# Attention and a quantized feed-forward on one core: two key tiles as one pattern of the matmul queue, and VectorE pinned to the order of the source

## The chip, the cores and the metric

The kernel runs on one NeuronCore of a Trainium2 chip. The metric is the device time of one execution in microseconds (us), the median of three runs. The engines are TensorE (PE in the profile, with its weight loads as PEld), VectorE (DVE), ScalarE (ACT), GpSimd (POOL) and SyncE (SP, which here only issues DMAs). They run side by side and wait for one another through semaphores. TensorE writes its results to PSUM[...]; VectorE and ScalarE read them there.

## What is computed

One transformer block in fp32: attention with 16 heads of 16 values over 4 sequences of 2048 rows, a residual and a layer norm, then a gated feed-forward whose activations and weights are rounded to a 4-bit grid in blocks of 16, a residual and a layer norm.

```python
q, k, v = split_heads(x @ Wq.T), split_heads(x @ Wk.T), split_heads(x @ Wv.T)   # x: 4 x 2048 x 256
attn = softmax(q @ k.T / sqrt(16))
x = layernorm(x + merge_heads(attn @ v) @ Wo.T)
gate, up = fp4(x) @ fp4(w_gate).T, fp4(x) @ fp4(w_up).T                         # 256 -> 704
x = layernorm(x + fp4(silu(gate) * up) @ fp4(w_down).T)                         # 704 -> 256
```

fp4(t) divides each block of 16 by a sixth of its largest absolute value, rounds to the nearest of 0, 0.5, 1, 1.5, 2, 3, 4, 6 with the sign kept, and multiplies back.

## The kernel before

**Tiles.** Attention is split into 64 steps (b, qb, g): one sequence, 512 query rows, four of the 16 heads. A step goes over 16 tiles of 128 keys, so the main loop has 1024 periods, one per key tile. The loop variable n counts periods from -20 to 1025.

**A period.** Three streams are in flight at once, at different steps:

- *maxima* (20 periods ahead, LEAD): scores of 128 queries against 512 keys for all four heads, in two halves i. Each half is two matmuls (the two heads of a pair, in rows 0 to 61 and 64 to 125 of the array) into a tile pm of two PSUM banks, and VectorE takes the row maxima of both (L432).
- *exponentials*: scores of 128 keys against 512 queries, with the row maximum folded in through two extra rows, so 64 rows per head. One matmul and one bank per head (pe); ScalarE takes the exponential of each bank into an SBUF tile e (L466).
- *values* (2 periods behind, LAG): four matmuls of 32 columns, one per head, into one bank av that adds up over the step.

The source's order for TensorE in a period is: both halves of the maxima, the exponentials' matmuls of the first pair, the values, the exponentials' matmuls of the second pair, and then one *part*.

**Parts.** All other work is cut into parts, written as generators: each runs to its next `yield` and gives a cost; a cost of at least 300 (LEAST) uses up the period's budget of one part (two before n = 0). Parts come from `urgent` (max_rows, which turns the maxima into the extra rows: its transposes are called pn; normalize, which divides by the softmax sums: pa, and pr for every second step) and from `queue`. The queue holds, for each block of 512 rows: the output projection (residual, py), the projection of a block of the next sequence (project: transposes ptx, then k and q in pq, v in pv), the transposes of the rounded x (ptq), gate and up (pg, pu), the transposes of the rounded hidden rows (pth) and the down projection (pz). A part that only waits yields LEAST and so uses a turn.

**Steps off TensorE.** `later(periods, step, rest)` puts a step into `due`; `take_due` runs it when its period has come, and a caller can ask whether it was done at least `rest` periods ago. fp4 takes block maxima, scales and multiplies, and rounds one period later; it works on VectorE and GpSimd. layer_norm takes its moments on VectorE (bn_stats, L524) and the rest on GpSimd.

**Order.** Every matmul and transpose is pinned to the source's order by `tc.keep_in_program_order`. Instructions of the other engines are ordered by the framework's scheduler, by its own estimate of when each is ready. The scheduler also picks the buffer that a tile gets and puts in the waits.

**Banks.** pm has two tiles of two banks (pool ps_m), av one bank (ps_av), and everything else, pe and all parts, shares three banks (pool ps_x, tag px, function psum).

**The end.** After the loop what is left of the parts is drained, and feed_forward_last does the last 512 rows with most of its steps on VectorE (fp4_at_once).

The main loop's core:

```python
for i in range(NP):
    if m < N:
        maxima(sm, im, i)
for i in range(NP):
    if 0 <= n < N:
        exponentials(s, kt, i)
    if i == 0 and n >= LAG:
        values(sv, kv)
...
period(1 if n >= 0 else 2)
```

Of the kernel before, what the change touches and what calls it, by code (L numbers as in the profile page):

```python
# [53 lines left out]
E_BUFS = 10  # L55
# [17 lines left out]

@with_exitstack
def block_kernel(
# [12 lines left out]
    nc = tc.nc  # L88
    B, L, D = x.shape
# [56 lines left out]
    def fp4(pool, t, tag, gain=1.0):  # L146

        p, nb, _ = t.shape
        amax = pool.tile([p, nb], F32, tag="amax" + tag, name="amax")
        nc.vector.tensor_reduce(amax, t, AX.X, ALU.max, apply_absolute_value=True)  # L150
        sc = pool.tile([p, nb], F32, tag="sc" + tag, name="sc")
        nc.vector.tensor_scalar(sc, amax, gain / 6.0, 1e-12, ALU.mult, ALU.max)
        rs = pool.tile([p, nb], F32, tag="rs" + tag, name="rs")
        nc.vector.reciprocal(rs, sc)
        nc.gpsimd.tensor_scalar(rs, rs, gain * TIES_DOWN, 1.0, ALU.mult, ALU.mult)
        xn = pool.tile([p, nb, FB], F32, tag="xn" + tag, name="xn", bufs=3 if tag else 2)
        nc.gpsimd.tensor_tensor(xn, t, rs.unsqueeze(2).to_broadcast([p, nb, FB]), ALU.mult)

        def rounded():
            m = pool.tile([p, nb, FB], F32, tag="m" + tag, name="m", bufs=1)  # L160
            nc.vector.tensor_single_scalar(m.bitcast(I32), xn.bitcast(I32), EXPONENT, ALU.bitwise_and)
            nc.vector.tensor_scalar(m, m, 1.0, ROUND, ALU.max, ALU.mult)  # L162
            nc.gpsimd.tensor_tensor(xn, xn, m, ALU.add)  # L163
            nc.gpsimd.tensor_tensor(xn, xn, m, ALU.subtract)  # L164
            nc.gpsimd.tensor_tensor(xn, xn, sc.unsqueeze(2).to_broadcast([p, nb, FB]), ALU.mult)  # L165

        return xn, later(1, rounded, 4 if tag == "" else 2)

    def fp4_at_once(pool, t, tag, gain=1.0):

        step = nc.vector
        p, nb, _ = t.shape
        amax = pool.tile([p, nb], F32, tag="amax" + tag, name="amax")
        step.tensor_reduce(amax, t, AX.X, ALU.max, apply_absolute_value=True)
        sc = pool.tile([p, nb], F32, tag="sc" + tag, name="sc")
        step.tensor_scalar(sc, amax, gain / 6.0, 1e-12, ALU.mult, ALU.max)
        rs = pool.tile([p, nb], F32, tag="rs" + tag, name="rs")
        step.reciprocal(rs, sc)
        step.tensor_scalar(rs, rs, gain * TIES_DOWN, 1.0, ALU.mult, ALU.mult)
        xn = pool.tile([p, nb, FB], F32, tag="xn" + tag, name="xn", bufs=3 if tag else 2)  # L180
        step.tensor_tensor(xn, t, rs.unsqueeze(2).to_broadcast([p, nb, FB]), ALU.mult)
        m = pool.tile([p, nb, FB], F32, tag="m" + tag, name="m", bufs=1)
        step.tensor_single_scalar(m.bitcast(I32), xn.bitcast(I32), EXPONENT, ALU.bitwise_and)
        step.tensor_scalar(m, m, 1.0, ROUND, ALU.max, ALU.mult)
        step.tensor_tensor(xn, xn, m, ALU.add)
        step.tensor_tensor(xn, xn, m, ALU.subtract)
        step.tensor_tensor(xn, xn, sc.unsqueeze(2).to_broadcast([p, nb, FB]), ALU.mult)
        return xn
# [14 lines left out]
    vt = [const.tile([P, NG, QT // 2, NP, 3 * DH], F32, tag=f"vt{i}", name=f"vt{i}") for i in range(4)]  # L203
# [40 lines left out]
    def turn_w(name, dst):  # L244
        for kc in range(KC):
# [3 lines left out]
            if name == "wv":  # L249
                nc.vector.tensor_copy(dst[:, kc, :], pt[:, :D])  # L250
                continue

            for n in range(KC):
                nc.vector.tensor_copy(
                    dst[:, kc, n * P : (n + 1) * P].rearrange("p (d h) -> p d h", h=NC),
                    pt[:, n * P : (n + 1) * P].rearrange("p (h d) -> p d h", h=NC),
                )
# [7 lines left out]
    def prepare():  # L265
# [10 lines left out]
        yield 500  # L276
# [37 lines left out]
        for piece, after in zip(pieces, pieces[1:] + [None]):  # L314
# [3 lines left out]
            yield 500  # L318
# [14 lines left out]
    def project(b, tb, what):  # L333
# [7 lines left out]
        for kc in range(KC):  # L341
# [4 lines left out]
            yield 600  # L346
        for name, c in [(w[0], int(w[1])) for w in what if w != "v"]:
# [18 lines left out]
        for t in range(QT if "v" in what else 0):  # L366
            v = vt[(tb * 2 + t // 2) % 4]
            pv = psum("pv")
            for kc in range(KC):
                matmul(  # L370
                    pv[:, :D], xT[:, kc, t * P : (t + 1) * P], wvT[:, kc, :], start=(kc == 0), stop=(kc == KC - 1)
                )
            src = pv[:, :D].rearrange("p (g i j d) -> p g i j d", g=NG, i=NP, j=2)
            for j in range(2):
                nc.scalar.copy(v[:, :, t % 2, :, 2 * j * DH : (2 * j + 1) * DH], src[:, :, :, j, :])
            if t % 2:
                t0 = tb * QT + t - 1
                nc.sync.dma_start(
                    vx[b % 2][:, :, t0 : t0 + 2, :].rearrange("g p t c -> p g (t c)"),
                    v.rearrange("p g t i c -> p g (t i c)"),  # L380
                )
            if t == QT - 1:
                projected.add((b, tb, "v"))
            yield 900
# [32 lines left out]
    def maxima(s, n, i):  # L417
# [14 lines left out]
        nc.vector.tensor_reduce(mx_sb[s][:, t, 2 * i : 2 * i + 2, kb], pm, AX.X, ALU.max)  # L432

    def max_rows(s):

        nm = p2.tile([P, QT, HG], F32, tag="nm", name="nm")
        nc.vector.tensor_reduce(nm, mx_sb.pop(s), AX.X, ALU.max, negate=True)
        nh = p2.tile([P, QT, HG, 2], F32R, tag="nh", name="nh")
        nc.vector.tensor_copy(nh[:, :, :, 0], nm)
        nc.vector.tensor_tensor(nh[:, :, :, 1], nm, nh[:, :, :, 0].bitcast(F32), ALU.subtract)  # L440
# [17 lines left out]
    def exponentials(s, kt, i):  # L458
        kb, col = kt // QT, kt % QT * P
        pe = [psum("pe") for _ in range(2)]  # L460
        for j in range(2):
            rows = slice(R * j, R * j + R)
            matmul(pe[j], k_sb[s, i, kb][rows, col : col + P], q_sb[s, i][rows, :], start=True, stop=True)
        for j in range(2):
            e = p1.tile([P, QB], F32, tag="e", name="e", bufs=E_BUFS)
            nc.scalar.activation(e, pe[j], AF.Exp, scale=SCALE)  # L466
            e_sb[s, kt, 2 * i + j] = e
# [15 lines left out]
    def normalize(s):  # L483
# [11 lines left out]
        nc.vector.reciprocal(rd, pairs[:, :, :, 1:3, 0])  # L495
# [3 lines left out]
        for i in range(NP):  # L499
            nc.vector.tensor_tensor(  # L500
# [5 lines left out]
        yield 500  # L506
        if s % 2 == 0:
            return
        yield 0
# [6 lines left out]
        yield 500  # L516


    def layer_norm(r, t0, n):

        mv = p2.tile([P, n, 2], F32, tag="mv", name="mv")
        for t in range(n):
            st = p2.tile([P, 6], F32, tag="st", name="st")
            nc.vector.bn_stats(st, r[:, t0 + t, :])  # L524
            nc.vector.bn_aggr(mv[:, t, :], st)
# [10 lines left out]
    def residual(b, qb, x1, xq):  # L536

        for t in range(QT):
# [10 lines left out]
            if t % 2:  # L549
                layer_norm(x1, t - 1, 2)  # L550
                tiles = x1[:, t - 1 : t + 1].rearrange("p t (b f) -> p (t b) f", f=FB)
                later(3, lambda tiles=tiles: xq.append(fp4(p2, tiles, "")))
# [36 lines left out]
    def turned(hq, tiles, hT):  # L589
# [4 lines left out]
        for t in range(2):  # L594
# [4 lines left out]
            yield 500  # L599
# [8 lines left out]
        yield 500  # L608
# [11 lines left out]
    def feed_forward(b, qb, between):  # L620
# [13 lines left out]
        for kc in range(KC):  # L634
# [5 lines left out]
            yield 500  # L640
        hq = {}

        def gate(t):
# [3 lines left out]
            later(1, lambda: hq.update({t: fp4(p2, blocks, "h", gain=0.5)}))  # L647

        def out_rows(t):
            layer_norm(x1, t, 2)  # L650
            at = slice(qb * QB + t * P, qb * QB + (t + 2) * P)
            nc.sync.dma_start(out[b, at, :].rearrange("(t p) d -> p t d", p=P), x1[:, t : t + 2, :])
# [25 lines left out]
    def feed_forward_last(b, qb, x1):  # L678
# [8 lines left out]
        def moments(t):  # L687
            st = p2.tile([P, 6], F32, tag="st", name="st")
            nc.vector.bn_stats(st, x1[:, t, :])
            mv = p2.tile([P, 4, 2], F32, tag="mv", name="mv")  # L690
            nc.vector.bn_aggr(mv[:, 0, :], st)
# [5 lines left out]
        def normed(t):  # L697
            mv, rstd = norms.pop(t)
            nc.vector.tensor_scalar(
# [3 lines left out]
        def attended(t):  # L703
# [5 lines left out]
            nc.vector.tensor_add(x1[:, t, :], x1[:, t, :], py[:, :D])  # L709
# [30 lines left out]
        def hidden(t):  # L740
            h = p2.tile([P, FF], F32, tag="h", name="h")
            for half, (a, g, u) in enumerate(gates.pop(t)):
                nc.vector.scalar_tensor_tensor(a, a, 1.0, g, ALU.add, ALU.mult)
                nc.vector.tensor_mul(h[:, half * FH : (half + 1) * FH], a, u)
# [23 lines left out]
        def added(t, pz):  # L768
            nc.vector.tensor_add(x1[:, t, :], x1[:, t, :], pz[:, :D])
# [49 lines left out]
    def period(parts):  # L819

        take_due()
# [6 lines left out]
        while parts > 0 and queue:  # L828
            parts -= (part(queue) or 0.0) >= LEAST
# [30 lines left out]
    for n in range(-LEAD, N + LAG):  # L860
        m = n + LEAD
        (sm, im), (s, kt), (sv, kv) = divmod(m, NKT), divmod(n, NKT), divmod(n - LAG, NKT)
# [6 lines left out]
        if n == N - NKT:  # L869
            x1_last = load_last(*steps[-1][:2])  # L870
# [13 lines left out]
        for i in range(NP):  # L884
            if m < N:
                maxima(sm, im, i)
        for i in range(NP):
            if 0 <= n < N:
                exponentials(s, kt, i)
            if i == 0 and n >= LAG:  # L890
                values(sv, kv)
        if m < N and im == NKT - 1:
            urgent.append(max_rows(sm))
        if n >= LAG and kv == NKT - 1:
            urgent.append(normalize(sv))
            if sv % NG == NG - 1 and sv + 1 < len(steps):
                queue.append(chain(*steps[sv][:2]))
        period(1 if n >= 0 else 2)
    banks["more"] = True
    while urgent or queue or due:  # L900
        period(1)
# [33 lines left out]
```

## Time and profile before

| | us |
|---|---|
| median of three runs | 3654.88 |
| lowest, highest | 3651.22, 3658.14 |
| the profiled execution's own time | 3651.45 |
| its span, first to last instruction | 3649.4 |

Its stages, as busy time of each engine in four stretches of the span:

```profile
core 0: us, PE busy (x) PEld busy (x) DVE busy (x) ACT busy (x) POOL busy (x), PEclk, DMA share, GB/s
0.00:110.00 110.00, 85.11 (x414) 54.45 (x414) 61.56 (x64) 45.77 (x120) 16.34 (x32) 0.94 0.69 222
110.00:300.00 190.00, 169.29 (x978) 71.41 (x977) 139.55 (x167) 130.49 (x274) 65.87 (x70) 0.92 0.44 136
300.00:3560.00 3260.00, 3218.46 (x19735) 1431.91 (x19727) 2564.48 (x2950) 2489.53 (x4995) 1160.50 (x1378) 1.00 0.28 85
3560.00:3650.00 90.00, 61.27 (x231) 35.98 (x231) 50.65 (x131) 25.25 (x60) 8.54 (x16) 0.85 0.02 6
```

Each line gives a stretch, its length, and for each engine the time in which it had an instruction running; PEclk is the share of TensorE's full clock that was granted. The first 110 us load and project, up to 300 us the weights of the feed-forward are rounded and transposed beside the first attention steps, from there to 3560 us the pattern repeats for every block of 512 queries (64 periods), and the last 90 us are feed_forward_last. In a timeline each line is a group of like instructions in a row: start, time from the first start to the last end, engine, source line, operation, out<-in, shapes (rows*columns of the array for matmuls), how many. Matmul ends are modelled by the profiler, so starts tell more than lengths. Nearly all matmuls have line L135, that of the helper; the name of the tile tells which they are.

### The profile page before, as it was taken

What the parts mean: (1) busy time and instruction counts of PE and PEld (TensorE: products, weight loads), DVE (VectorE), ACT (ScalarE), POOL (GpSimd) and SP (SyncE); (2) the same over time, 40 slices, a digit from 0 to 9 for tenths busy, and PEclk for the clock granted to TensorE, in tenths of its full rate; (3) what the DMA queues carried; (4) which work ended last, traced back from release to release, by engine and by line L of the source; (5) the groups of instructions that cost most, each with busy time, mean ns of one, the idle gap of its engine ahead of it and who ended that gap; (6) DMA issues with size and microseconds to landing.
All of it is one profiled execution on the core that took longest, in us unless ns stands there. A gap on an engine that the chain in (4) does not pass through costs nothing.

```text
span 3649.4 us, 57772 instructions
## 1 busy us (share of the span) xinstructions
PE 3534.1 (97%) x21348; PEld 1593.8 (44%) x21348; DVE 2816.2 (77%) x3310; ACT 2691.0 (74%) x5446; POOL 1251.3 (34%) x1496
## 2 busy tenths in 40 slices
PE   7889999999999999999999999999999999999996
PEld 5333444444444444444444444444443434444343
DVE  5777778787787778778787787878778787888845
ACT  3677777777777777777777777777777777777772
POOL 1331423434243242424324243342424325142430
PEclk9999999999999999999999999999999999999998
DMA  6533323323232322323223232322322221222100
GB/s 219 164 123 99 119 68 113 89 85 103 82 98 87 105 84 83 116 68 116 85 85 106 80 100 86 97 85 83 109 69 77 67 84 50 86 66 81 57 21 6
DMA packets 190640, 328.39 MB, mean 90 GB/s; under 512 B 24344, under 2 KB 68248, under 8 KB 190360
## 3 DMA queue, kind: packets, MB, share of 16 engines
q1 hardware_dynamic: 188968, 323.39, 29.1%
q8 instruction: 171, 2.80, 0.3%
q10 hardware_dynamic: 1392, 1.31, 0.1%
q14 instruction: 109, 0.89, 0.1%
HBM read 237.04 MB, written 86.51 MB: 89 GB/s over the span
## 4 chain that ended last, share of the span: by engine, by line
PE 82%; DVE 12%; DMA 2%; POOL 2%; issue 1%; ACT 1%; SPq 0%; POOLq 0%; ACTq 0%; DVEq 0%
PE av L135 24%; PE pe L135 18%; PE pm L135 16%; DVE mx L432 9%; PE pz L135 6%; PE pg L135 5%; PE pu L135 5%; PE pq L135 3%; PE pv L135 2%; PE pth L138 1%; PE pa L138 1%; PE py L135 1%; PE pn L138 1%; DMA qx<-qhi 1%; DVE st L524 1%
## 5 line engine op out<-in xcount | busy, mean ns | idle before, releaser
L432 DVE TENSOR_REDUCE mx<-pm 128x2 f32<-128x1024 f32 x2048 | 2408.6, 1217 | 666.5 <-PE pm L135 662.2
L466 ACT ACTIVATE e<-pe 128x512 f32<-128x512 f32 x4096 | 2218.8, 596 | 676.0 <-PE pe L135 670.8
L135 PE MATMUL av<-e,v 128*32 128x512 f32 x8192 | 1098.0, 608 | 4.2 <-DMA v<-vx 4.2
L135 PE MATMUL pe<-q,k 64*128 64x512 f32 x4096 | 1036.4, 456 | 4.9 <-ACT e L466 4.5
L135 PEld LDWEIGHTS pe<-q,k 64*128 64x128 f32 x4096 | 476.6, 184 | 968.5 <-ACT e L466 853.8
L135 PE MATMUL pm<-k,q 62*128 62x512 f32 x4096 | 805.1, 448 | 67.1 <-DVE mx L432 57.5
L135 PEld LDWEIGHTS pm<-k,q 62*128 62x128 f32 x4096 | 346.8, 185 | 382.7 <-DVE mx L432 178.2
L135 PEld LDWEIGHTS av<-e,v 128*32 128x32 f32 x8192 | 162.1, 108 | 335.5 <-issue 312.9
L572 POOL TENSOR_TENSOR a<-a,g 128x352 f32<-128x352 f32 x120 | 112.6, 938 | 494.5 <-ACT a L571 494.5
L135 PE MATMUL pz<-wdT,hT 128*128 128x128 f32 (+1 forms) x1488 | 233.4, 299 | 1.5 <-ACT hT L757 1.5
L617 POOL TENSOR_TENSOR x<-x,read 128x128 f32<-128x128 f32 x120 | 54.8, 456 | 482.2 <-ACT read L143 482.2
L135 PEld LDWEIGHTS pz<-wdT,hT 128*128 128x128 f32 x1488 | 190.5, 193 | 50.5 <-ACT e L466 18.2
L163 POOL TENSOR_TENSOR xn<-xn,m 128x704 f32<-128x704 f32 (+2 forms) x100 | 153.6, 1536 | 153.5 <-DVE m L162 131.6
L586 POOL TENSOR_TENSOR h<-a,u 128x352 f32<-128x352 f32 x120 | 112.4, 937 | 226.0 <-ACT u L585 224.0
L135 PE MATMUL pg<-wgT,xqT 128*128 128x352 f32 x512 | 186.5, 487 | 1.9 <-ACT xqT L720 1.9
L135 PE MATMUL pu<-wuT,xqT 128*128 128x352 f32 x512 | 185.0, 484 | 0.0
L548 POOL TENSOR_TENSOR x<-x,read 128x256 f32<-128x256 f32 x60 | 43.8, 730 | 374.0 <-ACT read L143 374.0
L164 POOL TENSOR_TENSOR xn<-xn,m 128x704 f32<-128x704 f32 (+2 forms) x100 | 153.8, 1538 | 5.4
L165 POOL TENSOR_TENSOR xn<-xn,sc 128x704 f32<-128x704 f32 (+2 forms) x100 | 126.4, 1264 | 7.5
L573 POOL TENSOR_TENSOR a<-a,g 128x352 f32<-128x352 f32 x120 | 113.9, 949 | 9.4
L135 PEld LDWEIGHTS pg<-wgT,xqT 128*128 128x128 f32 x512 | 87.5, 190 | 60.2 <-ACT e L466 19.1
L135 PEld LDWEIGHTS pu<-wuT,xqT 128*128 128x128 f32 x512 | 87.6, 189 | 58.1 <-ACT e L466 20.0
(114 smaller groups left out, 2278.8 us busy)
## 6 DMA issues: line engine op xcount, KB each, us to landing
k<-kx SPq DMA_DIRECT2D x1024, 128.0 KB
v<-vx SPq DMA_DIRECT2D x64, 768.0 KB
q<-qx SPq DMA_DIRECT2D x256, 124.0 KB
kx<-khi SPq DMA_DIRECT2D x64, 256.0 KB
qx<-qhi SPq DMA_DIRECT2D x64, 256.0 KB
vx<-vt SPq DMA_DIRECT2D x32, 384.0 KB
xb<-in_L_attn_x_dram SPq DMA_DIRECT2D x16, 512.0 KB
kx<-klo SPq DMA_DIRECT2D x32, 256.0 KB
```

Source lines behind the costliest of these rows:

```text
L135: tc.keep_in_program_order(nc.tensor.matmul(*args, **kw))
L138: tc.keep_in_program_order(nc.tensor.transpose(*args))
L163: nc.gpsimd.tensor_tensor(xn, xn, m, ALU.add)
L164: nc.gpsimd.tensor_tensor(xn, xn, m, ALU.subtract)
L165: nc.gpsimd.tensor_tensor(xn, xn, sc.unsqueeze(2).to_broadcast([p, nb, FB]), ALU.mult)
L432: nc.vector.tensor_reduce(mx_sb[s][:, t, 2 * i : 2 * i + 2, kb], pm, AX.X, ALU.max)
L466: nc.scalar.activation(e, pe[j], AF.Exp, scale=SCALE)
L548: nc.gpsimd.tensor_add(x1[:, t, :], x1[:, t, :], read(py[:, :D]))
L572: nc.gpsimd.tensor_mul(a, a, g)
L573: nc.gpsimd.tensor_add(a, a, g)
L586: nc.gpsimd.tensor_mul(h[:, cols], a, u)
L617: nc.gpsimd.tensor_add(x1[:, t, cols], x1[:, t, cols], read(pz))
```

## The change

- **One pattern for two periods.** The loop goes in steps of 2, and the order of the two periods is written out in ORDER: m and n are halves of the maxima of the first and second period, e and f the exponentials of one head each, v and w the values, q and r the places for parts. `exponentials` now takes one head instead of a pair.
- **Both parts at q.** `more(2)` runs two parts one after the other at q. A part that yields TIED (the last transposes before matmuls that read them: xT, xqT, hT) ends the run of parts, and what is left of the budget is taken at r. max_rows and normalize run up to their first `yield` where they are begun.
- **VectorE pinned.** `vector = InOrder(tc, nc.vector)` replaces nc.vector everywhere, so every VectorE instruction keeps the source's order. Due steps are taken after m1 and after n1, that is, behind those maxima.
- **Later due times.** fp4 has a step of its own for the scales, one period after the block maxima, and rounds after three periods instead of one; layer_norm in residual and out_rows comes two periods later; the quantization after it four periods later instead of three; that of the hidden rows three instead of one.
- **Buffers and order.** E_BUFS 12 for 10; three staging tiles vt for four; the projection's parts come in the order k0, q0, v, k1, q1 instead of v last; normalize loses one empty `yield`.

```diff
+ORDER = "m0 e0 m1 e1 q e2 n0 e3 v n1 f0 f1 r f2 w f3".split()
+TIED = 500.0
-E_BUFS = 10
+E_BUFS = 12
...
+class InOrder:
+    def __init__(self, tc, engine):
+        self.tc, self.engine = tc, engine
+
+    def __getattr__(self, name):
+        return lambda *args, **kw: self.tc.keep_in_program_order(getattr(self.engine, name)(*args, **kw))
...
+    vector = InOrder(tc, nc.vector)
...
-        return xn, later(1, rounded, 4 if tag == "" else 2)
+        later(1, scaled)
+        return xn, later(3, rounded, 4 if tag == "" else 2)
...
-    def exponentials(s, kt, i):
+    def exponentials(s, kt, h):
+        i, j = divmod(h, 2)
         kb, col = kt // QT, kt % QT * P
-        pe = [psum("pe") for _ in range(2)]
-        for j in range(2):
-            rows = slice(R * j, R * j + R)
-            matmul(pe[j], k_sb[s, i, kb][rows, col : col + P], q_sb[s, i][rows, :], start=True, stop=True)
-        for j in range(2):
-            e = p1.tile([P, QB], F32, tag="e", name="e", bufs=E_BUFS)
-            nc.scalar.activation(e, pe[j], AF.Exp, scale=SCALE)
-            e_sb[s, kt, 2 * i + j] = e
+        pe = psum("pe")
+        rows = slice(R * j, R * j + R)
+        matmul(pe, k_sb[s, i, kb][rows, col : col + P], q_sb[s, i][rows, :], start=True, stop=True)
+        e = p1.tile([P, QB], F32, tag="e", name="e", bufs=E_BUFS)
+        nc.scalar.activation(e, pe, AF.Exp, scale=SCALE)
+        e_sb[s, kt, h] = e
...
-    def period(parts):
-        take_due()
+    def more(parts):
         for _ in range(len(urgent)):
...
         while parts > 0 and queue:
-            parts -= (part(queue) or 0.0) >= LEAST
+            cost = part(queue) or 0.0
+            parts -= cost >= LEAST
+            if cost == TIED:
+                break
+        return parts
...
+    for n in range(-LEAD, N + LAG, 2):
+        left = 0
+        for step in ORDER:
+            n_of = n + (step[0] in "nfwr")
+            m = n_of + LEAD
+            if step in ("m0", "n0"):
+                loads(n_of)
+            if step[0] in "mn" and m < N:
+                maxima(*divmod(m, NKT), int(step[1]))
+                if step == "n1" and (m + 1) % NKT == 0:
+                    begin(max_rows(m // NKT))
+            if step in ("m1", "n1"):
+                take_due()
+            if step[0] in "ef" and 0 <= n < N:
+                exponentials(*divmod(n_of, NKT), int(step[1]))
+            elif step in "vw" and n >= LAG:
+                s, kt = divmod(n_of - LAG, NKT)
+                values(s, kt)
+                if kt == NKT - 1:
+                    begin(normalize(s))
+                    if s % NG == NG - 1 and s + 1 < len(steps):
+                        queue.append(chain(*steps[s][:2]))
+            elif step == "q":
+                left = more(2)
+            elif step == "r" and n < 0:
+                more(2)
+            elif step == "r":
+                while left > 0 and queue:
+                    left -= (part(queue) or 0.0) >= LEAST
```

## The prediction

> **What bounds the kernel now.** I read the page's busy shares first, then the idle time in the costliest groups, and last the timeline of two kinds of period.
>
> ```profile
> span 3649.4 us, 57772 instructions
> ...
> PE 3534.1 (97%) x21348; PEld 1593.8 (44%) x21348; DVE 2816.2 (77%) x3310; ACT 2691.0 (74%) x5446; POOL 1251.3 (34%) x1496
> ...
> L135 PE MATMUL pe<-q,k 64*128 64x512 f32 x4096 | 1036.4, 456 | 4.9 <-ACT e L466 4.5
> ...
> L135 PE MATMUL pm<-k,q 62*128 62x512 f32 x4096 | 805.1, 448 | 67.1 <-DVE mx L432 57.5
> ```
>
> TensorE is the bound: its matmuls stand still for 4.9 us before all exponentials' scores and 67.1 us before all maxima's scores. But 97% busy is not 97% useful, and the timeline says why. A period with a heavy part (starts in us, then length):
>
> ```profile
> 1506.25 0.74 PE L135 MATMUL pm<-k,q 62*128 62x512 f32 x4
> ...
> 1506.81 0.42 PE L135 MATMUL pe<-q,k 64*128 64x512 f32 x2
> ...
> 1507.16 1.07 PE L135 MATMUL av<-e,v 128*32 128x512 f32 x8
> ...
> 1508.15 0.50 PE L135 MATMUL pe<-q,k 64*128 64x512 f32 x2
> ...
> 1508.58 1.45 PE L135 MATMUL pg<-wgT,xqT 128*128 128x352 f32 x4
> ...
> 1509.96 0.73 PE L135 MATMUL pm<-k,q 62*128 62x512 f32 x4
> ```
>
> Read the starts, as the lengths overlap. Four pm take 0.56 us, that is two pairs: the two heads of a pair sit in rows 0 to 61 and 64 to 125 and run side by side, in one slot of about 0.227 us (start of a second pair to what follows it). A pair of pe alone costs 1508.58 - 1508.15 = 0.43, not 0.23: it stands between two changes of array shape (32 columns, 64 rows, 128 rows). So a stretch of one shape costs some 0.2 us beside its slots. The start of the run prices it apart: eight pv in a row take 1.93 us to the next start (38.54 to 40.47), while four of the same size between changes take 1.06 (pq, 1505.19 to 1506.25). 2 x 1.06 - 1.93 = 0.19 per stretch.
>
> ```profile
> 38.54 1.99 PE L135 MATMUL pv<-wvT,xT 128*128 128x256 f32 x8
> 40.47 0.74 PE L135 MATMUL pm<-k,q 62*128 62x512 f32 x4
> ```
>
> A period has four stretches (pm pm pe | av | pe | part), 0.7 to 0.8 us of 3.4. A period with a light part:
>
> ```profile
> 1782.77 0.66 PE L138 MATMUL pth<-ident,xn 128*128 128x128 f32 x4
> ...
> 1782.87 1.09 ACT L466 ACTIVATE e<-pe 128x512 f32<-128x512 f32 x2 [0.53 <-PE pe L135]
> ...
> 1783.36 0.73 PE L135 MATMUL pm<-k,q 62*128 62x512 f32 x4
> ...
> 1783.92 0.58 PE L135 MATMUL pe<-q,k 64*128 64x512 f32 x2
> ...
> 1784.44 1.06 PE L135 MATMUL av<-e,v 128*32 128x512 f32 x8
> ```
>
> Here pe to av takes 0.52, against 0.35 in the heavy period: the second pe waits for a bank until ScalarE has finished the exponentials that it began at 1782.87 (three px banks for five uses a period). That is 0.18 us in each of some 20 light periods in 64.
>
> The last thing to see is how far rows are independent:
>
> ```profile
> 1818.06 0.50 PE L135 MATMUL pm<-k,q 62*128 62x512 f32 x1
> 1818.26 0.27 PE L135 MATMUL pz<-wdT,hT 64*128 64x128 f32 x1
> 1818.29 0.71 PE L135 MATMUL pm<-k,q 62*128 62x512 f32 x3
> ```
>
> The last pz, in rows 0 to 63, stands before every pm in the source, yet a pm (of the upper rows) began 0.2 us before it.
>
> [...]
>
> **The change, part by part.** I count one iteration (two periods) and a block of 32 iterations (64 periods, one block of queries; 218.6 us in the trace), then multiply by 13: the 3260 us of steady state are 14.9 blocks, and the last three carry no projection.
>
> 1. *Stretches.* Before, two periods have 8. After: f3 m0 e0 m1 e1 | q's parts | e2 n0 e3 | v | n1 f0 f1 f2 | w, so 6 when both parts stand at q and r is empty. Saved: 2 x 0.195 = 0.39 us. Following the queue through a late block with its due times, 25 of 32 iterations have two parts at q; four are split by TIED into q and r, three have one part or none (the longer due times, 2+4+3+4 periods from the last py to a usable xq against 3+1+4, make the queue wait five or six turns). In these seven both kernels have about equally many stretches. 25 x 0.39 = -9.8.
> 2. *Lost pairs.* Before, 16 matmuls of 64 rows an iteration fill 8 slots. After, counting lower rows A and upper rows B: first stretch 3 A and 4 B (4 slots), second 2 and 2 (2 slots), third 3 and 2 (3 slots), if A and B run independently as at 1818. 9 slots, one more: 32 x 0.227 = +7.3. In strict order the second stretch takes e2, then n0, then e3: 3 slots, 10 in all.
> 3. *Light parts.* Scores come one by one, so ScalarE gets its work spread out; but two light parts now sit together and need 8 exponentials and 2 copies in one shorter iteration. Bounds: the 20 x 0.18 = 3.6 us stay, or go. I take half: -1.8.
> 4. *VectorE's order.* The block has about 2.2 us where TensorE waits for VectorE's maxima (0.97 us at 1670, where two normalizations and an amax stood ahead; the rest in periods without a part). Pinning the maxima ahead of the later steps removes none or all; half: -1.1.
> 5. *New: q's first part behind f3.* Its bank is f3's. From f3 to that part are 4 x 0.227 + 0.2 = 1.11 us; the exponential is ready at 0.44 (pe to ACT in the trace) + 0.60 + about 0.1 for the release = 1.14. Bounds 0 and 0.1; I take 0.05: 25 x 0.05 = +1.2.
> 6. *New: pa.* normalize's reciprocal and two products read pa's bank and are now pinned behind both maxima of m0 and m1 and the step due there, and n0's maxima stand behind them on VectorE. Maxima m0 and m1 end about 0.62 + 2 x 1.14 = 2.9 us after f3, the three readers add 0.26 + 2 x 0.29 = 0.84: bank free at 3.8. e3 wants its bank at 2.9 (heavy second part) or 2.1 (light). If it needs pa's bank it waits 0.9 to 1.7, and 1.2 more where a rounding (0.58 + 0.60) was due; if it may take the other part's bank, about nothing. Four a block; I take 0.4 each: +1.6.
> 7. *Nothing.* E_BUFS 12: e's life grows to 12 tiles, and the same 12 are there. vt 3: TensorE's next pv comes long after the vx store (SP's queue sees the same DMAs, loads earlier in the iteration by up to a period). The projection's v parts only move forward. POOL at 34% carries the same work; if its results came late, the pinned rounding would hold the maxima, but three periods lie between. The last feed-forward block (90 us) pins VectorE's order there too: its idle gaps of 2 to 5 us wait for TensorE in both; +-8 us, taken as nothing.
>
> Sum per block: -9.8 + 7.3 - 1.8 - 1.1 + 1.2 + 1.6 = -2.6; x 13 = -34 us. The profiled execution has 3651.45 us (span 3649.4, about 2 us around it), so 3617; the median of the runs shown is 3654.88, 3 us higher, so 3620.
>
> **Rivals.**
> - *More is gained* (0.13): the light waits and the stalls on maxima go fully, items 5 and 6 cost nothing: 1.8 + 1.1 + 1.2 + 1.6 = 5.7 more a block, 74 us: 3545. For it: ScalarE at 74% and VectorE at 77% have room. Against: two parts together make bursts.
> - *Strict order on TensorE* (0.15): the second stretch takes one slot more. Where TensorE binds, 25 x 0.227 x 13 = +74: 3694, slower. [...] Against: 1818.06.
> - *pa holds the bank* (0.18), on the slower side: one mechanism, at e3 behind q's first part, 64 times in the run. At its full price, 1.5 us on average, 64 x 1.1 beyond the 0.4 charged = +70: 3690. It turns the sign from 0.4 + 34/64 = 0.93 us a time. For: three banks, and every pa is the first part at q. Against: before, the wait for the reciprocal is hidden, and another bank may be free.
> - *It cancels* (0.07): stretches and slots come out even, 3650.
>
> **How the numbers follow.** The likeliest case, 0.47, gives 3620, own range 3595 to 3645 (items 3 to 6 at either half). About 0.2% (7 us) is what a measurement here tells from no change. Faster: nearly all of 0.47 plus 0.13, 0.58; within 0.2%: the cancelling case and edges, 0.09; slower: 0.33. The range 3560 to 3700 leaves out half of the large gain and the upper third of the two slower cases.
>
> **What would show it.** Right: two parts in one stretch with some 0.2 us less than apart; e2 and the upper half of n0 starting together; m0 with f3 starting together. Wrong: e2, n0, e3 in three slots of 0.227; PE idle at e3 "<-DVE oq" near 1 us 64 times; idle at q's first part "<-ACT e" over 0.1; waits of pm for maxima grown because a pinned step waits for POOL; no-part iterations above 5.4 us. The forecast is wrong if the iteration with two heavy parts is not shorter than 7.41 us, twice 3.71.

## The result, and the profile after

| | before | after |
|---|---|---|
| median, us (runs) | 3654.54 (6) | 3679.74 (6) |
| lowest, highest | 3651.22, 3658.14 | 3673.23, 3681.60 |
| span of the profiled execution | 3649.4 | 3677.4 |

The kernel became slower: ratio 1.0066, 95% interval 1.0053 to 1.0079. The forecast was 3620. The page after, first its span and busy shares, then the three costliest groups that matter here (busy time, mean ns | idle time before them and what ended most of it):

```profile
span 3677.4 us, 57767 instructions
...
PE 3543.7 (96%) x21348; PEld 1647.0 (45%) x21348; DVE 2844.1 (77%) x3310; ACT 2644.7 (72%) x5446; POOL 1248.5 (34%) x1495
...
L490 ACT ACTIVATE e<-pe 128x512 f32<-128x512 f32 x4096 | 2188.3, 602 | 527.9 <-PE pe L151 471.7
L151 PE MATMUL pe<-q,k 64*128 64x512 f32 x4096 | 1313.3, 426 | 5.3 <-DVE oq L86 2.0
L151 PE MATMUL pm<-k,q 62*128 62x512 f32 x4096 | 1128.0, 453 | 53.5 <-DVE mx L86 43.3
```

TensorE is still the bound, and by this page its maxima's scores wait less for VectorE's maxima than before (43.3 us against 57.5, of 53.5 and 67.1 in all). Nothing here explains 28 us more, so the loss must be read from stages and single iterations. The stages, as windows over the span:

```profile
core 0: us, PE busy (x) PEld busy (x) DVE busy (x) ACT busy (x) POOL busy (x), PEclk, DMA share, GB/s
...
300.00:3560.00 3260.00, 3193.15 (x19499) 1460.19 (x19500) 2570.44 (x2928) 2423.25 (x4953) 1152.17 (x1361) 0.99 0.28 85
3560.00:3678.00 118.00, 85.96 (x373) 50.88 (x372) 60.01 (x140) 35.93 (x85) 19.19 (x36) 0.84 0.03 9
```

In the same 3260 us TensorE issued 19499 matmuls, where before it issued 19735. Set period against period by the start of the values' matmuls, the kernel after is 15.5 us ahead at period 384, loses 1 to 2.5 us in each block of 64 periods from there to 768, then 3.9, 7.3 and 8.4 us in the next three, and leaves the loop 14.9 us late. From the last values to the end it takes 91.4 us, before 78.3: 13.1 us more.

What the pattern does well is seen in an iteration with two heavy parts. The timeline of TensorE (start, length to the last end):

```profile
1544.13 0.49 PE L151 MATMUL pe<-q,k 64*128 64x512 f32 x1
1544.13 0.73 PE L151 MATMUL pm<-k,q 62*128 62x512 f32 x2
...
1545.31 1.45 PE L151 MATMUL pg<-wgT,xqT 128*128 128x352 f32 x4
1546.60 1.35 PE L151 MATMUL pu<-wuT,xqT 128*128 128x352 f32 x4
1547.88 0.50 PE L151 MATMUL pe<-q,k 64*128 64x512 f32 x1
1547.88 0.73 PE L151 MATMUL pm<-k,q 62*128 62x512 f32 x2
1548.22 0.39 PE L151 MATMUL pe<-q,k 64*128 64x512 f32 x1
1548.54 1.06 PE L151 MATMUL av<-e,v 128*32 128x512 f32 x8
...
1551.43 0.49 PE L151 MATMUL pe<-q,k 64*128 64x512 f32 x1
```

f3 and a half of m0 start together at 1544.13, e2 and a half of n0 at 1547.88 (the upper-row one, I infer, as e2 and the other half share the lower rows), and from e2 to the values there are 0.66 us: two slots of 0.227 and a change of shape, not three slots. So the upper and the lower rows run independently here. pg and pu together take 2.57 us, two single ones 2 x 1.38. The iteration takes 7.30 us where twice 3.71 stood: 0.11 gained, just the 0.39 - 0.227 - 0.05 of the forecast. But only 77 of 480 iterations hold such a pair of pg and pu. An iteration whose first part is pa:

```profile
1525.26 1.44 PE L151 MATMUL pg<-wgT,xqT 128*128 128x352 f32 x4
1526.63 0.50 PE L151 MATMUL pe<-q,k 64*128 64x512 f32 x1
1526.64 0.73 PE L151 MATMUL pm<-k,q 62*128 62x512 f32 x2
1527.54 0.47 PE L151 MATMUL pe<-q,k 64*128 64x512 f32 x1 [0.17 <-DVE oq L86]
1527.94 1.07 PE L151 MATMUL av<-e,v 128*32 128x512 f32 x8
```

Here the same stretch takes 1.31 us, as e3 gets pa's bank only after normalize's last product. The bracket names the right culprit, but its 0.17 is only what is left when the modelled end of the pm before it is taken off: read the starts.

A last look at the parts: hidden rows' transposes that wait for GpSimd. Before, no wait of these transposes for GpSimd is on record.

```profile
3163.82 0.66 PE L154 MATMUL pth<-ident,xn 128*128 128x128 f32 x4
3163.91 1.39 POOL L183 TENSOR_TENSOR xn<-xn,sc 128x704 f32<-128x704 f32 x1
3165.25 0.71 POOL L551 TENSOR_TENSOR rstd<-rstd,minus_half 128x2 f32<-128x2 f32 x1
...
3165.35 0.66 PE L154 MATMUL pth<-ident,xn 128*128 128x128 f32 x4 [0.87 <-POOL xn L183]
```

The rounding's last product ends at 3165.3; TensorE waited for it 0.87 us. The windows around that place:

```profile
3163.00:3166.00 3.00, 1.98 (x13) 1.21 (x13) 2.36 (x3) 1.56 (x3) 2.79 (x5) 1.00 0.91 261
3166.00:3170.00 4.00, 4.00 (x18) 1.25 (x17) 1.60 (x2) 1.75 (x4) 1.09 (x2) 0.57 0.30 105
3170.00:3173.50 3.50, 3.50 (x26) 1.86 (x26) 2.56 (x3) 3.17 (x7) 0.00 (x0) 1.00 0.47 144
```

After a stretch in which TensorE was busy 1.98 of 3 us, its granted clock was 0.57 over 4 us. From 330 us on the trace of after has eight such episodes in the loop, that of before two.

### The profile page after: what moved, and what is told of

Its sections match the earlier page's. It is cut to its first block, busy times and chain, and to the rows that moved or that the text cites. A ratio compares the mean times of both kernels' runs of the same rounds, so it can differ in the third digit from the quotient of the medians.

```text
span 3677.4 us, 57767 instructions
## 1 busy us (share of the span) xinstructions
PE 3543.7 (96%) x21348; PEld 1647.0 (45%) x21348; DVE 2844.1 (77%) x3310; ACT 2644.7 (72%) x5446; POOL 1248.5 (34%) x1495
## 3 DMA queue, kind: packets, MB, share of 16 engines
q10 hardware_dynamic: 1392, 1.31, 0.1%
## 4 chain that ended last, share of the span: by engine, by line
PE 81%; DVE 11%; ACT 5%; DMA 2%; POOL 1%; issue 1%; SPq 0%; POOLq 0%; ACTq 0%; DVEq 0%
PE av L151 24%; PE pe L151 18%; PE pm L151 14%; DVE mx L86 7%; PE pz L151 5%; PE pu L151 4%; PE pg L151 4%; ACT e L490 3%; PE pq L151 3%; PE pv L151 2%; PE py L151 2%; PE pth L154 1%; DVE m L86 1%; PE pn L154 1%; PE pa L154 1%
## 5 line engine op out<-in xcount | busy, mean ns | idle before, releaser
L86 DVE TENSOR_REDUCE mx<-pm 128x2 f32<-128x1024 f32 x2048 | 2437.7, 1220 | 681.8 <-PE pe L151 513.3
L490 ACT ACTIVATE e<-pe 128x512 f32<-128x512 f32 x4096 | 2188.3, 602 | 527.9 <-PE pe L151 471.7
L151 PE MATMUL pe<-q,k 64*128 64x512 f32 x4096 | 1313.3, 426 | 5.3 <-DVE oq L86 2.0
L151 PE MATMUL pm<-k,q 62*128 62x512 f32 x4096 | 1128.0, 453 | 53.5 <-DVE mx L86 43.3
L151 PEld LDWEIGHTS pe<-q,k 64*128 64x128 f32 x4096 | 610.9, 187 | 680.6 <-ACT e L490 487.2
L151 PEld LDWEIGHTS pm<-k,q 62*128 62x128 f32 x4096 | 486.9, 186 | 547.5 <-issue 236.2
L159 ACT COPY read<-pz 128x128 f32<-128x128 f32 x120 | 31.9, 266 | 135.6 <-PE pm L151 83.1
```

The source lines that it names most:

```text
L86: return lambda *args, **kw: self.tc.keep_in_program_order(getattr(self.engine, name)(*args, **kw))
L151: tc.keep_in_program_order(nc.tensor.matmul(*args, **kw))
L159: nc.scalar.copy(t, bank)
L490: nc.scalar.activation(e, pe, AF.Exp, scale=SCALE)
```

## The experiments

All ratios are to runs of the kernel before on the same chip, with 95% intervals. The experiments ran on several chips, on which the kernel before had medians from 3651.6 to 3655.7 us, so differences of a few us between two experiments are safer by the ratios than by the medians.

**The two halves apart.** The change is an order for TensorE and a discipline for VectorE (pinning and due times). Each alone (of the due times only the rounding's is shown; the others went with it. The buffers go with the order; the projection's new order of parts, v ahead of k1 and q1, is in both):

```diff
 e9_order_alone (after)
-    vector = InOrder(tc, nc.vector)
+    vector = nc.vector
-        later(1, scaled)
-        return xn, later(3, rounded, 4 if tag == "" else 2)
+        scaled()
+        return xn, later(1, rounded, 4 if tag == "" else 2)
...
 e10_vector_alone (before)
+    vector = InOrder(tc, nc.vector)
-        return xn, later(1, rounded, 4 if tag == "" else 2)
+        later(1, scaled)
+        return xn, later(3, rounded, 4 if tag == "" else 2)
...
```

> The order half of the change alone: after's order of matmuls and of parts, VectorE not pinned, and the due times of before. Theory A (the new order leaves the maxima less room, n0 needing the tile that m0's maxima free, so it depends on the VectorE half): 3740 to 3790 us, as when only the pinning was taken away (3777). Rival B (that loss came from unpinned VectorE together with the later due times, so the order half alone does as forecast): 3620 to 3690 us.

> The VectorE half of the change alone on the order of matmuls of before: all of VectorE pinned, the later due times, and values projected ahead of k1 and q1 as these due times need. Pinning alone cost 48 us on this order; on the order of after the later due times were worth 26. Theory A (the half is a loss here or nothing): 3660 to 3685 us, of which 8 in the last feed-forward. Rival B (with both parts the maxima's waits go, some 60 us): below 3640 us, and the loss of the change lies in its order of matmuls.

| us (ratio) | VectorE as before | VectorE as after |
|---|---|---|
| order as before | 3654 | 3653.35 (1.0000, 0.9991 to 1.0009) |
| order as after | 3786.54 (1.0365, 1.035 to 1.0381) | 3679.74 (1.0066, 1.0053 to 1.0079) |

The VectorE half is worth nothing on the old order and 107 us on the new one; the order loses with either. e10 met neither of its two ranges: its trace leaves the loop 10 us ahead of before and needs 13 us more than before from the last values to the end. Why the order alone is so slow stands in its waits (total, times, longest):

```profile
PEld pm L151 <- DVE mx L457: 284.0, 288, 6.5
...
PE pm L151 <- DVE mx L457: 112.4, 104, 6.2
```

After has 155.9 and 43.3 there, before 178.2 and 57.5. In the new order n0 follows m0 within one iteration and needs the pm tile that m0's maxima free, so a step that gets ahead of a maximum on VectorE can be paid on TensorE.

Parts of the VectorE half were taken away singly: the pinning in the new order (e2), the later due times in the new order (e7), and pinning without later due times in the old (e8).

```diff
 e2_dve_free (after)
-    vector = InOrder(tc, nc.vector)
+    vector = nc.vector
 e7_early_due (after)
-        later(1, scaled)
-        return xn, later(3, rounded, 4 if tag == "" else 2)
+        scaled()
+        return xn, later(1, rounded, 4 if tag == "" else 2)
...
 e8_before_pinned (before)
+    vector = InOrder(tc, nc.vector)
```

> The changed kernel with VectorE left to the scheduler everywhere. Theory 'pinning costs': the tail's 8 us come back, and in the loop the waits of TensorE that begin with a pinned step (0.45 us at each of 64 pa, and pm waiting behind rounding steps in iterations without parts) shrink: 3640 to 3665. Rival 'pinning protects the maxima and the loss is the new pattern of the matmul queue': the loop stays or grows, because due steps get ahead of the maxima again: 3670 to 3690.

> After, with the due times of the steps of before (scaling and layer norm at once, fp4 3 periods behind, the rounding 1, the hidden rows' fp4 1), all else as in after, VectorE still pinned. Theory A: TensorE's 22 us of waits for GpSimd's xn ahead of pth, and part of the half-clock episodes that follow them, come from the later due times: 3645 to 3665 us. Rival B (the later due times are what keeps VectorE's order clear of the maxima): the waits for GpSimd go but pm waits for VectorE grow by more: 3680 to 3700 us.

> The kernel before, with VectorE's instructions pinned to the source's order and nothing else changed. Theory A (pinning alone is a small gain in the loop, where maxima were overtaken, and a loss of about 8.6 us in the last feed-forward): 3645 to 3665 us. Rival B (pinning without the later due times stalls VectorE behind waits for GpSimd, and the maxima behind it): 3670 to 3720 us. Rival C (the maxima's waits go, some 60 us): below 3620 us, which would put the loss of the change at its order of matmuls.

e2: 3777.87 us (1.0344, 1.0329 to 1.036), a miss of both its theories by some 90 us: without the pinning the new order is nearly as slow as in e9. e7: 3705.33 us (1.0138, 1.0123 to 1.0153), 26 us slower than after: its rival B, 5 us above its range, and GpSimd's waits ahead of pth did go. e8: 3701.76 us (1.013, 1.0115 to 1.0145): pinning without the later due times costs 48 us on the old order. In its trace VectorE waits 46.4 us for GpSimd's sums ahead of layer_norm's moments (3.9 in before), the maxima pinned behind these steps are held with them, and the matmuls of pm wait 86.3 us for VectorE's maxima (57.5 in before). On the new order the pinning is worth 81 us with the early due times (e9, e7) and 98 with the later ones (e2, after); the later due times are worth 9 us without the pinning and 26 with it. So what each is worth depends on the other, and pinning is a loss only on the old order with early due times. Later due times without pinning on the old order were not run.

**The order, varied.** One part at q and one at r (e5), f2 behind w, which makes eight slots of nine (e4), and a pz that stands first at q with its 64-row chunk first (e6):

```diff
 e5_parts_apart (at q, and the same line at r in place of what stood there)
-                left = more(2)
+                more(2 if n < 0 else 1)
...
 e4_f2_behind_w
-ORDER = "m0 e0 m1 e1 q e2 n0 e3 v n1 f0 f1 r f2 w f3".split()
+ORDER = "m0 e0 m1 e1 q e2 n0 e3 v n1 f0 f1 r w f2 f3".split()
 e6_pz_rows
-            for c in range(NFC):
+            chunks = list(range(NFC)) if row["n"] else [NFC - 1, *range(NFC - 1)]
+            for c in chunks:
...
```

> After, with the same order of matmuls but one part of the queue at q and one at r (in place of two at q and r as a reserve). Theory A (the pattern pays where two parts join, but less than forecast): each iteration with two parts gets a 64-row stretch more (about 0.2 to 0.4 us with its ends), so over some 400 such iterations the loop loses 80 to 170 us and gives back at most some 40 us of waits behind light parts: 3710 to 3800 us. Rival B (two parts in a row are themselves the loss: light pairs and pa hold the banks): 3640 to 3670 us.

> The changed kernel with f2 moved behind w, next to f3: the 64-row matmuls then fill 8 slots an iteration in place of 9, with the same number of stretches. If slots are what the pattern costs: 480 x 0.227 less, down to 3571. If the three px banks are: q's first part waits for the bank of an exponential that starts half a microsecond later than now; about 0.5 us more at each of some 430 parts, less the slot: 3680 + 430 x 0.27 = about 3800. Which of the two shows says whether the slot lost was worth its price.

> After, with the chunks of a pz part that stands first at q computed in another order: its 64-row chunk first, beside the 64-row stretch ahead of it, instead of last. Theory A: in after a pair of pz parts costs 0.19 us more than two single ones, since the first one's 64-row chunk stands alone between two 128-row ones; about 30 pairs and 30 mixed ones save 0.2 to 0.4 us each, so 6 to 15 us: 3665 to 3674 us against 3680. Rival B (the switch isn't what the pair pays): within 3 us of after.

e5: 3796.27 us (1.039, 1.0375 to 1.0406). Two parts in a row are worth 116 us in this order, so they aren't the loss. e4: 3759.36 us (1.0297, 1.028 to 1.0314). It saves the slot and loses 80 us more than after, the way that its second mechanism said, if not as much. Its timeline shows why:

```profile
1550.99 0.50 PE L151 MATMUL pe<-q,k 64*128 64x512 f32 x2
1551.33 0.40 PE L151 MATMUL pm<-k,q 62*128 62x512 f32 x2
1551.56 0.40 PE L151 MATMUL pe<-q,k 64*128 64x512 f32 x1
1551.57 0.63 PE L151 MATMUL pm<-k,q 62*128 62x512 f32 x2
1552.26 0.50 PE L151 MATMUL pe<-q,k 64*128 64x512 f32 x1
1552.75 1.45 PE L151 MATMUL pg<-wgT,xqT 128*128 128x352 f32 x4
```

f2, f3, e0 and e1 now stand in one stretch, four uses of three banks: e1 starts 0.70 us after e0 where a slot is 0.227. In the whole trace the weight loads of pe wait 644.7 us for ScalarE's exponentials, in after 487.2. Here the three banks, not the slots, limit how many scores can stand together.

e6: 3669.14 us (1.0039, 1.0025 to 1.0053), 10.6 us faster than after by the medians and 10 by the ratios. The pair of pz in after, and below it in e6:

```profile
1189.87 3.41 PE L151 MATMUL pz<-wdT,hT 128*128 128x128 f32 x23 [0.28 <-ACT e L490]
1192.92 0.49 PE L151 MATMUL pm<-k,q 62*128 62x512 f32 x1
1193.12 0.27 PE L151 MATMUL pz<-wdT,hT 64*128 64x128 f32 x1
```

```profile
1189.64 3.22 PE L152 MATMUL pz<-wdT,hT 64*128 64x128 f32 x23 [0.28 <-ACT e L491]
1192.50 0.49 PE L152 MATMUL pm<-k,q 62*128 62x512 f32 x1
1192.70 0.27 PE L152 MATMUL pz<-wdT,hT 64*128 64x128 f32 x1
```

Each pz ends with a chunk of 64 rows. Single, as in all of before, that chunk joins the scores that follow; the first of a pair stands between 128-row matmuls and pays two changes of shape. From start to the next pm 3.05 us became 2.86: the 0.19 of one stretch. So two pz in a row cost about 0.2 us more than two apart.

**Urgent parts, and the end.** The urgent part second (e3), and VectorE free in the last feed-forward (e1):

```diff
 e3_pa_second (in more, ahead of the urgent parts)
+        while parts > 1 and queue and urgent and cost < LEAST:
+            cost = part(queue) or 0.0
+            parts -= cost >= LEAST
...
 e1_tail_free (fp4_at_once, feed_forward_last)
-        step = vector
+        step = nc.vector
+        vector = nc.vector
```

> The changed kernel with one queue part ahead of the urgent one at q, so that pa's bank is wanted by f0 and not by e3. If e3 waits for pa's bank (S3 stretch 1.03 to 1.30 us after a pa against 0.66 after pg and pu): the stretch goes back to about 0.67, 64 x 0.45 = 29 us less, about 3651. If another cause holds e3 (the VectorE queue itself): nothing changes, 3680.

> The changed kernel with VectorE left to the scheduler in feed_forward_last alone (and in fp4_at_once, which only it calls). In the traces the time from the first residual sum there to the end grew from 73.0 to 81.6 us. If the pinned order is what costs there: 8 to 9 us less than the changed kernel, about 3671, and the stretch is back at 73. If the growth comes from what the drained parts leave behind (late sums on GpSimd, a slow clock): no change, 3680.

e3: 3670.89 us (1.0057, 1.0042 to 1.0072), 9 us less by the medians, but only 3 by the ratios, whose intervals overlap; 29 had been expected. The stretch behind pa and pu fell from 1.03 to 0.67 us, as it should; but with a pz in first place (31 times) its chunk now stood in the middle at some 0.3 us each. e1: 3671.78 us (1.0052, 1.0037 to 1.0067), 8 us less by the medians and 5 by the ratios, whose intervals overlap too. Its trace has 81.7 us from the last values to the end, where after has 91.4.

**Put together.** e13 is after with e1, e3 and e6. e11 has besides one part at every other q in the last sequence, e15 at every fourth, and e12 and e14 take e11 and e13 with the rounding one period earlier and the transposes of the hidden rows one period further behind it:

```diff
 e11_combined
-                left = more(2)
+                left = more(2 if n < 3 * NQB * NG * NKT + 72 or n % 4 else 1)
 e15_three_sp8
+                left = more(2 if n < 3 * NQB * NG * NKT + 72 or n % 8 else 1)
 e12_comb_rest, e14_three_rest
-        return xn, later(3, rounded, 4 if tag == "" else 2)
+        return xn, later(2, rounded, 4 if tag == "" else 3)
```

> After, with four edits: VectorE free in the last feed-forward (8 us by its own run), one queue part ahead of the urgent one (9 us, and the 31 x 0.3 us it lost ahead of a pz), a pz first at q starting with its 64-row chunk (11 us), and in the last sequence one part at every other q (last blocks 4 to 8 us each slower than before, three of them). If these are the causes and add: 3680 - 8 - 9 - 9 - 11 - 8 = 3635 us, range 3625 to 3648, faster than before's 3652. If they overlap, or moving parts off some q's costs what it saves: 3650 to 3665.

> The run before it, with the rounding due 2 periods behind the scaling in place of 3 and the hidden rows' transposes 3 behind it in place of 2, so that GpSimd has one period more. If the lateness of GpSimd (22 us of TensorE's waits, and the half-clock episodes behind them) is a cause of its own: 8 to 25 us faster than that run. If the waits are hidden by what follows, or the earlier rounding steps on the maxima: within 5 us of it, or slower.

> After with three edits (VectorE free in the last feed-forward; one queue part ahead of the urgent one; a pz first at q starts with its 64-row chunk). Up to period 768 the loop should stand where it stood with four edits, 20 to 23 us ahead of before; the blocks from 768 on lose 15 to 20 us as in after; the tail is about 82 us against 78. If these three and the last sequence are the causes: 3645 to 3656 us, equal to before. If they don't add: 3660 or more.

> As e13, with the rounding due 2 periods behind the scaling in place of 3, and the hidden rows' transposes 3 behind it in place of 2. If GpSimd's lateness is a cause of its own: 6 to 15 us faster than e13. If the earlier rounding only moves the wait to the maxima (the same edit stood 10 us behind at period 768 in the pair of runs before): 3 to 12 us slower than e13.

> As e13, with one part in place of two at every fourth q of the last sequence (57 places a block of 64 periods for 46 to 50 parts, so none should be left over). If two parts at a q whose chain is not ready, and the idle gaps behind them, are what the last blocks lose: 5 to 12 us faster than e13. If pace only moves parts: within 5 us, with a longer tail.

| | us | ratio | out of the loop against before, us | last values to the end, us |
|---|---|---|---|---|
| e11 | 3677.38 | 1.0066 (1.005 to 1.0082) | -39.4 | 142.5 |
| e12 | 3662.20 | 1.0027 (1.0017 to 1.0037) | -23.5 | 113.4 |
| e15 | 3660.81 | 1.0015 (1.0009 to 1.0022) | -16.5 | 104.4 |
| e13 | 3652.24 | 0.9990 (0.9982 to 0.9999) | -7.9 | 82.2 |
| e14 | 3641.30 | 0.9963 (0.995 to 0.9976) | -8.6 | 76.9 |

e11 was a miss, and the last column tells why: fewer places for parts near the end only push them behind the loop, where nothing stands beside them. e15, with fewer such places, missed the same way: 9 us slower than e13. e12's figure against e11 is mixed with that, so e13 and e14 decide. e13: the three edits together give back what the change lost against before, 27.5 us by the medians and 28 by the ratios. Singly they gave 8 + 9 + 10.6 = 27.6 us by the medians, but 5 + 3 + 10 = 18 by the ratios, so whether they simply add isn't decided. Nor do they bring the forecast gain of 34 us: e13 stands level with before. e14 is 11 us faster than e13, by medians; the two traces differ by 6 us, of which 5.3 are in the tail, where e13 has three pz left over behind the loop and e14 none. In the loop the waits for GpSimd ahead of pth are gone (14.1 us on the weight loads in e13, no such row in e14), but weight loads of pm wait 185.6 us for maxima in place of 151.5, and the mean granted clock of the profiled execution is 0.988 in place of 0.989. Its stages:

```profile
300.00:3560.00 3260.00, 3205.78 (x19712) 1486.71 (x19712) 2584.55 (x2942) 2441.23 (x4992) 1159.00 (x1376) 1.00 0.28 85
3560.00:3640.00 80.00, 52.65 (x195) 32.37 (x193) 50.62 (x131) 18.52 (x46) 10.52 (x21) 0.85 0.03 10
```

19712 matmuls in the 3260 us against 19499, and 80 us left where after has 118. e14 is faster than before and after. What the old order gives with the same care at the end:

```diff
 e16_vector_tail (e10)
-        step = vector
+        step = nc.vector
+        vector = nc.vector
```

> The VectorE half of the change on before's order of matmuls (as in e10), with VectorE free in the last feed-forward. If the half is a gain of 10 us in the loop given back in the pinned tail: 3642 to 3648 us, faster than before. If the tail's 14 us come from late due times and not from the order: 3650 to 3655 us.

3646.45 us (0.9977, 0.9971 to 0.9984). So VectorE's half, with its tail mended, is a gain of 9 us without any new order, and e14, the repaired new order, is only 5 us better than that. These 5 us can't be put down to the order: e14 also has other due times for the rounding, which were not tried on the old order, and e13, with the due times of e16, is 6 us slower than e16.

## Why the prediction was wrong

The table sets the forecast, times the 15 blocks from period 64 on, against the two traces. I took the time from the start of each stretch of one shape to the next; the lower quartile of its kind is its ordinary length, the rest its waits.

| us, after less before | steps of the forecast | forecast | measured |
|---|---|---|---|
| 64-row stretches, ordinary length | half of 1, 2, 5 | +54 | +43.5 |
| 64-row stretches, waits | 3, 4, 6 | -19.5 | -2.8 |
| 128-row stretches, ordinary length | half of 1 | -73 | -35.8 |
| 128-row stretches, waits | 7 | 0 | +10.7 |
| 32-column stretches | none | 0 | +3.0 |
| up to period 64 | none | 0 | -5.5 |
| last values to the end | 7 | 0 | +13.1 |

The rows add to +26 of the 28 us between the spans; the traces miss a few matmul records. The forecast column adds to -39, its 13 blocks to -34. Steps 1 and 7 failed, and iterations with no part were missing from the sum; the other steps came nearer to their size.

- *Stretches (1)* failed in its half for parts. "25 x 0.39" put the 0.19 of the best pair on every pair. pg with pu, pq with pq, py with py and pv with pg do save 0.20. But pa with pu saves 0.10 and pn with pu 0.05, pth with pth 0.12 to 0.18, and pz with pz costs about 0.2. Of the 372 pairs in the trace from period 64 on, 157 are of two such heavy parts, pz left out. The number of pairs, 25 a block, was right. Of the 35.8 us another 4.6 are parts that were put off. The step forgot that a pz ends in 64 rows, though the forecast's own last fence shows one. e6 gave about 10 us of this back. This is the step that failed most: 73 us were forecast from it in this row of the table, and 35.8 came.
- *Lost pairs (2)* and *q's first part (5)* were right: nine slots, and 0.07 us at q (1.18 us from f3 to the part, 1.11 without a wait). *Strict order on TensorE*, the rival, is shown wrong: the upper-row half of n0 starts with e2, ahead of the lower-row half that stands before it in the source, in at least 330 of the 393 stretches of this kind.
- *Light parts (3)* and *VectorE's order (4)*: waits fell by about as much as *pa (6)* added. pa's 0.4 was right, about 0.45 us a time and 29 us in all; taken off, the other waits fell by some 32 us, from 95 to 63, where 43 were forecast. The rival in which pa holds the bank needed 0.93 a time and didn't decide; e3 had back 3 to 9 us of it.
- *Nothing (7)* failed twice. "Three periods lie between" held for rounding and maxima, but not for the hidden rows' transposes: GpSimd was busy 34% of the time, yet its last product came so late that weight loads of pth stood idle up to 1.7 us. And the end, "+-8 us, taken as nothing", took 13.1: by its trace e1 puts 9.7 of them down to the pinned order, and the trace of after puts 3.5 us on three pz left over, the first residual sum beginning 5.6 us after pr in place of 2.1.
- *Missing from the sum*: iterations with no part. The forecast named them as a sign of being wrong (above 5.4 us), but priced them at nothing: "about equally many stretches". Their stretch "f3 m0 e0 m1 e1 e2 n0 e3" takes 2.78 us at the median, as n0 waits for m0's maxima, and such an iteration 5.67 us, where twice 2.69 stood. Over the 39 of them from period 64 on the mean is 6.09, and 23 stand in the last sequence, where with 46 parts a block places stay empty and 20 us were lost.

One such iteration shows what stands ahead of the maxima even with VectorE pinned:

```profile
1496.38 0.22 DVE L86 TENSOR_REDUCE nm<-mx 128x16 f32<-128x64 f32 x1
...
1497.27 0.42 DVE L86 TENSOR_SCALAR m<-xn 128x512 int32<-128x512 int32 x1
...
1498.07 3.48 DVE L86 TENSOR_REDUCE mx<-pm 128x2 f32<-128x1024 f32 x3
...
1499.34 0.50 PE L151 MATMUL pm<-k,q 62*128 62x512 f32 x2 [1.20 <-DVE mx L86]
```

max_rows and a rounding, both begun behind n1, stand on VectorE ahead of the next m0's maxima for 1.7 us (1496.38 to 1498.07), and TensorE waits 1.20 us at n0. Each block between periods 384 and 768 has one such iteration. Behind four of these six, this one among them (0.50 from 1500.45 to 1503.86), the clock is halved: the iteration then takes 7.96 us in place of 6.43 or so, and the block 221.1 us in place of 219.5, where before needs 218.6. So an episode costs about 1.5 us, and an estimate from these pairs puts 9 of the 28 us down to the six episodes that after has more than before.

The test that the forecast named for itself, two heavy parts under 7.41 us, was met at 7.30, and the kernel was slower all the same: it tested the best iteration, not the sum.

## What to carry to other kernels

When a pattern merges stretches, price every kind of pair that will really stand together, from the shapes of its first and last instruction, and multiply by how often it occurs; one representative pair says little. Price the emptiest iteration of the pattern too: with no part beside them, the waits for VectorE lay open. An order of one engine and the discipline of another can be one change: alone the first cost 133 us here and the second nothing, so measure the four combinations before judging either. Follow deferred work to the end of the program: what the loop sheds comes back where nothing covers it (39 us ahead out of the loop, 64 us behind in the tail).

## What the runs showed of the hardware

- A TensorE that was busy only 1.98 of 3 us, in waits of about 0.4 and 0.9 us, then ran at about half its clock (0.57 over 4 us; eight values' matmuls took 1.9 us in place of 1.0). In the clock records of after each of the eight episodes in the loop from 330 us on lasts 3.41 us, at a clock of 0.50; in the 3.41 us ahead of each the clock was 1.00 and TensorE was busy 1.97 to 2.22 us (58 to 65%), with no gap over 1.5 us. Such a stretch didn't always bring the drop: the like wait of 1.21 us that ended at 1720.42, with TensorE busy 2.19 us (64%) from 1717.50 to 1720.90, was not followed by one (clock 1.00 from there to 1740).
- In these traces a change of shape cost a stretch of one matmul as much as one of four: 0.19 us for the 64-row chunk inside a pair of pz, measured directly as 3.05 less 2.86, and 0.19 us between eight pv in a row and two fours apart (2 x 1.06 less 1.93).
